# The MLP's second matrix product by two levels of seven products, with its weight operands formed during the attention

## The chip, the cores and the metric

The kernel is one program on one NeuronCore of a Trainium2 chip. The metric is the time of one execution on the device in microseconds (us). Three runs of the kernel before took 3018.52, 3020.32 and 3024.05 us; the median is 3020.32. All data are float32.

A core has a matrix engine (TensorE, PE in the profile; the loads of its stationary operand are listed as PEld), a vector engine (VectorE, DVE), a scalar engine (ScalarE, ACT), a general engine (GpSimd, POOL) and an engine that here only issues transfers (SyncE, SP). Each has its own queue and works through it in order. They meet through semaphores. SBUF is the working memory with 128 partitions, PSUM holds the results of matrix products, and DRAM holds inputs, outputs and scratch tensors.

## The reference

Two layers. The first is a graph attention over 4 x 1024 rows of 512 features with 20 key rows per batch; nothing in it is changed. The second is a transformer block on the result, conditioned by a vector per batch:

```python
mod = jax.nn.silu(c) @ W_mod + b_mod
sh_msa, sc_msa, g_msa, sh_mlp, sc_mlp, g_mlp = jnp.split(mod, 6, axis=-1)
x = x + g_msa * _attention(_modulate(_layernorm(x), sh_msa, sc_msa), W_qkv, W_out, b_out)
x = x + g_mlp * _ff(_modulate(_layernorm(x), sh_mlp, sc_mlp), W1, b1, W2, b2)
# _ff: gelu(x @ W1 + b1) @ W2 + b2, W1 512 x 2048, W2 2048 x 512
# _modulate: x * (1 + scale) + shift; 16 heads of 64; 4 batches of 1024 rows
```

The change is about `@ W2`, a product of 4096 x 2048 by 2048 x 512.

## The kernel before

**Stages.** The graph attention takes the first part, layer 1's attention the middle (about 471 to 2236 us of the profiled execution), the MLP the rest. The attention is a loop over `NS` = 256 steps. Beside each step's score and value products a planner places other work: `add(lo, hi, units, place, f, ...)` appends a task with the steps between which it is due, its share of a step and a rank in it. `emit` takes the tasks out at their steps and so fixes each engine's order. With every step POOL scales the softmax weights (L1219), DVE transposes them (L1228), SP writes them to DRAM (`wd`) and loads them back as `wT` for the value product (L1101).

**Products with seven parts.** Where a product has a 2 x 2 block form, `seven` and `with_four` (L558 to L610) form it from seven products of sums of blocks instead of eight of blocks (Strassen's method in Winograd's arrangement). Four PSUM banks `ma`, `mb`, `mc`, `md` take the seven in the order a, c, b, a2, b2, d, b3. Between them ACT copies `ma` into `mb` and `mc` into SBUF, and DVE forms `md` from `mb` and that copy (`start_d`, L585) and the last result from the same (`last`, L589); `done` takes each finished quarter. A product that reads a bank which another engine writes waits for it; `start_d` must be over before b2, `last` before b3.

**The MLP.** The rows are taken in `NB2` = 8 blocks k of 512 rows (`VB` = 4 tiles of 128). A block has two stages. In the up stage four units p, one level of seven each, form gelu(x @ W1 + b1) into `hs[p]`. A product is four matmuls of 128x256, and in this trace each float32 matmul appears as two records. ACT applies gelu from PSUM (L699), and `up_sums(p)` forms on DVE the sums of blocks of `hs` that the next stage needs (four operations of 128x512 into `hx[p]` and in place, L542 to L545). The down stage forms the block's `@ W2` by one level of seven: 16 matmuls of 128x256 a product, left operand from `hs` or `hx`, right operand a block of `w2s` (W2 in SBUF, four loads of 1 MB, L1601) or a sum of blocks `w2x` (formed once on DVE, eight operations of 128x1024, L550, in block 0). `dn_done` (L1687 to L1698) multiplies a quarter by the gate (L1690) and adds it to the rows (L1695); finished rows go out by SP.

Beside that, for the next block: `norm_load` fetches its rows (tile `xl`, queue SP) ahead of the up stage. `norm_rows` normalizes them on DVE behind unit 2 (L425). `between`, behind the first down product, transposes them in blocks of 32 on DVE (`norm_turn`, L465), and 16 transfers of 64 KB each place them in `hT`. In `between` the block's own rows are loaded too, and POOL adds the bias to them (L1680). `modulated`, behind the fourth product, applies scale and shift on ACT (`norm_mod`, L479), and POOL forms the sums of blocks of `hT` (`mlp_rows`, L550). Block 0 differs: its first two units run in the last steps of the attention, and the loads of `w2s` stand in SP's queue ahead of the rows of block 1.

Of the kernel before, what the change touches and what calls it, by code (L numbers as in the profile page):

```python
# [12 lines left out]
F32 = mybir.dt.float32  # L13
# [6 lines left out]
P = 128  # L20
# [21 lines left out]
def cond_block_kernel(  # L42
# [86 lines left out]
    x2d = [tc.dram_tile([P, F], F32, name=f"x2d{i}") for i in range(NTA)]  # L129


    with ExitStack() as gctx:
# [279 lines left out]
        def norm_load(st, k):  # L412
            for i in range(k * VB, (k + 1) * VB):
                t = rp.tile([P, F], F32, name="xl", tag="xl", bufs=VB)
                nc.sync.dma_start(t, NORM[st][0][i])
                xl[st, i] = t
# [44 lines left out]
        def norm_turn(st, k, n, home):  # L461

            hT[st, k] = hT[st, 0]
            t = home(n)
            nc.vector.transpose(  # L465
                t.rearrange("p (m k) -> p m k", k=RB),
                xl.pop((st, k * VB + n)).rearrange("p (m k) -> p m k", k=RB),
            )
            for u in range(P // RB):
                at = n * P + u * RB  # L470
                nc.sync.dma_start(hT[st, k][:, :, at : at + RB], t[RB * u : RB * (u + 1), :])

        def norm_mod(st, k, c):

            sh, sc = NORM[st][4:]
            b = k * VB // NT
            o = hT[st, k][:, c, :]
            scale, shift = modT[:, sc + c, b : b + 1], modT[:, sh + c, b : b + 1]
            nc.scalar.activation(o, o, AF.Identity, scale=scale, bias=shift)  # L479
# [74 lines left out]
        def sums_b(*args):  # L554
            for f in steps_b(*args):
                f()
# [111 lines left out]
        def mlp_rows():  # L668

            h = hT[1, 0]  # L670
            if "mlp" not in tx:
                tx["mlp"] = xp.tile([P, 6, F], F32, name="tx", tag="tx")
            o = [tx["mlp"][:, k, :].rearrange("p (c r) -> p c r", c=2) for k in range(3)]
            sums_b(nc.gpsimd, o, h[:, :2, :HB], h[:, :2, HB:], h[:, 2:, :HB], h[:, 2:, HB:])
# [26 lines left out]
        def up_sums(p):  # L701
            h = [hs[p][:, 2 * k : 2 * k + 2, :] for k in range(4)]
            sums_a(nc.vector, [hx[p][:, k] for k in range(3)], *h)


# [273 lines left out]
    with ExitStack() as actx:  # L979
# [273 lines left out]

        fill = []
# [5 lines left out]
        def add(lo, hi, units, place, f, *args):  # L1260
            fill.append((lo, hi, units, place, lambda: f(*args)))
# [96 lines left out]
        add(3, 3, 0, 4, rstd, rs1, mv1, nm1, NT, NTA)  # L1358

# [22 lines left out]
        add(NS - 8, NS - 8, 0, 4, mlp_rows)  # L1382
# [203 lines left out]
    with ExitStack() as mctx:  # L1586
# [12 lines left out]
        w2s = [mp2.tile([P, 4, F], F32, name=f"w2_{k}") for k in range(4)]  # L1599
        for k in (0, 2, 1, 3):  # L1600
            nc.sync.dma_start(w2s[k], w2[k * F : (k + 1) * F, :].rearrange("(c p) f -> p c f", p=P))  # L1601
        w2x = [mp2.tile([P, 3, 4, HB], F32, name=f"w2x{k}") for k in range(2)]
        for p in range(4):
            hx[p] = mp2.tile([P, 3, 2, HB], F32, name=f"hx{p}")
# [6 lines left out]
        gate2, bias2 = (tx["mlp"][:, k, :] for k in (3, 4))  # L1611

        def dn_lhs(which, t, c):
            p, q = divmod(c, 2)
            rows = slice(t * P, (t + 1) * P)
            at = {4: 0, 5: 1, 2: 2}.get(which)
            if at is not None:
                return hx[p][:, at, q, rows]
            return hs[p][:, 2 * {0: 0, 1: 1, 6: 2, 3: 3}[which] + q, rows]

        def dn_rhs(which, t, c):
            k, r = divmod(c, 4)
            at = {4: 0, 5: 1, 3: 2}.get(which)
            if at is not None:
                return w2x[k][:, at, r, :]
            h, f = {0: (0, 0), 1: (1, 0), 2: (1, 1), 6: (0, 1)}[which]
            return w2s[2 * h + k][:, r, f * HB : (f + 1) * HB]
# [4 lines left out]
        rows2 = {}  # L1632
        NB2 = NTA // VB
        for k in range(NB2):
# [4 lines left out]
            for p in range(2 if k == 0 else 0, 4):  # L1639
# [10 lines left out]
                if k > 0:  # L1650
                    up_sums(p)
                elif p == 3:
                    sums = []
                    for j in range(2):
                        o = [w2x[j][:, n] for n in range(3)]
                        q, r = w2s[j], w2s[2 + j]
                        sums.append(steps_b(nc.vector, o, q[:, :, :HB], q[:, :, HB:], r[:, :, :HB], r[:, :, HB:]))
                    for n, two in enumerate(zip(*sums)):
                        for f in two:
                            f()  # L1660
                        if n == 0:
                            up_sums(p)
                if p == 1 and k == 1:
                    rstd(rs2, mv2, nm2, 3 * NT, NTA)
                if p == 2 and nxt < NB2:
                    norm_rows(1, nxt)

            def between():
                if nxt < NB2:
                    for n in range(VB):  # L1670
                        norm_turn(1, nxt, n, lambda n: short() if n % 2 else tx["mlp"][:, 5, :])
                if k * VB % NT == 0:
                    spread(2, b, gate2)
                    spread(3, b, bias2)
                for n in range(VB):
                    i = k * VB + n
                    rows2[n] = rp.tile([P, F], F32, name="x2", tag="xl", bufs=VB)
                    nc.sync.dma_start(rows2[n], x2d[i])
                for n in range(VB):
                    nc.gpsimd.tensor_tensor(rows2[n], rows2[n], bias2, ALU.add)  # L1680

            def modulated():
                for c in range(FC):
                    norm_mod(1, nxt, c)
                mlp_rows()

            def dn_done(i, j, t):  # L1687
                y = t if (i, j) == (1, 1) else short()
                g = gate2[:, j * HB : (j + 1) * HB].unsqueeze(1).to_broadcast([P, 2, HB])
                nc.vector.tensor_tensor(  # L1690
                    y.rearrange("p (t f) -> p t f", t=2), t.rearrange("p (t f) -> p t f", t=2), g, ALU.mult
                )
                for n in range(2):
                    o = rows2[2 * i + n][:, j * HB : (j + 1) * HB]
                    nc.vector.tensor_tensor(o, o, y[:, n * HB : (n + 1) * HB], ALU.add)  # L1695
                    if (i, j) in ((0, 1), (1, 0)):
                        at = k * VB + 2 * i + n
                        nc.sync.dma_start(out[at * P : (at + 1) * P, :], rows2[2 * i + n])  # L1698

            steps = with_four(  # L1700
                get=dn_banks.get, short=short, lhs=dn_lhs, rhs=dn_rhs, nk=MC // 2, room=None, done=dn_done
            )
            for n, f in enumerate(steps):
                f()
                if n == 0:
                    between()
                if n == 3 and nxt < NB2:
                    modulated()
# [60 lines left out]
```

## Time and profile before

| | |
|---|---|
| median of three runs | 3020.32 us |
| profiled execution: its time, its span | 3032.2 us, 3030.2 us |
| granted TensorE clock, mean | 0.997 |
| PE busy | 2995.2 us, 99% |
| DVE, ACT, POOL busy | 67%, 48%, 44% |
| DMA: moved, mean rate | 425.25 MB, 140 GB/s |
| one MLP block, from one first down product to the next | 96.7 us |
| of it the seven down products | 7 x 6.91 us |

The page of a profile names groups of instructions by line, engine, operation, tiles and shape; each has its busy time, the mean of one in ns, and the idle time before it with what ended it. The chain of waits is followed back from the last instruction: start, length, engine, tile and line of each step. A timeline lists instructions in order with start and length (x n for a run of equal ones). A table of windows gives each engine's busy time in stretches of time. In the transfer view, digits are the busy tenths of the DMA engines in equal slices, with the GB/s moved under them.

### The profile page before, as it was taken

Reading aid. Unit: us, or ns where it says so; the run is one execution under the profiler, and the core shown is the slowest. Engines: PE = TensorE matmul, PEld = TensorE weight load, DVE = VectorE, ACT = ScalarE, POOL = GpSimd, SP = SyncE. Lnnn points to the kernel's source line nnn. Section 1 sums busy time; section 2 is a strip of 40 time slices with the busy share of each in tenths; the row PEclk is TensorE's granted clock in tenths of the full one; section 3 lists DMA queues with packets and bytes.
Section 4 is the critical chain, followed back from the end, with each engine's and each line's share of the span. In section 5 each row is a group of like instructions: output and inputs, shape, how many; then the busy total and the mean of one; then the engine's idle time right before and its main releaser. Section 6 shows DMA issues by size and latency. Waiting matters only on the chain.

```text
span 3030.2 us, 41832 instructions
## 1 busy us (share of the span) xinstructions
PE 2995.2 (99%) x15205; PEld 1969.9 (65%) x15205; DVE 2018.4 (67%) x2852; ACT 1441.5 (48%) x2380; POOL 1339.4 (44%) x922
## 2 busy tenths in 40 slices
PE   9999999999999999999999999999999999999999
PEld 6666665565555555555565555555568888888888
DVE  3788867787878877878887878887865332233222
ACT  2344456555755555755555755556641322222211
POOL 1444456555665655665665575664641101110110
PEclk8999999999999999999999999999999999999999
DMA  6343437776877776867776877876764212212020
GB/s 193 118 131 117 136 99 188 167 173 157 204 169 191 191 175 151 209 167 194 190 173 151 206 168 184 198 175 153 190 177 127 49 32 60 56 35 56 29 63 14
DMA packets 341833, 425.25 MB, mean 140 GB/s; under 512 B 88105, under 2 KB 160229, under 8 KB 341629
## 3 DMA queue, kind: packets, MB, share of 16 engines
q1 hardware_dynamic: 341392, 422.37, 55.2%
q8 instruction: 122, 2.00, 0.3%
q14 instruction: 83, 0.67, 0.1%
q10 hardware_dynamic: 236, 0.20, 0.0%
HBM read 120.93 MB, written 25.76 MB: 48 GB/s over the span
## 4 chain that ended last, share of the span: by engine, by line
PE 81%; DVE 7%; POOL 3%; issue 3%; DMA 3%; ACT 2%; SPq 2%; POOLq 0%; DVEq 0%; ACTq 0%
PE q L571 18%; PE psc L1193 14%; PE pav L1101 13%; PE pu L1176 6%; PE mbd L571 5%; PE mbu L571 5%; PE mad L571 4%; PE mau L571 3%; PE mdd L571 2%; PE mcd L571 2%; PE mdu L571 2%; PE mcu L571 2%; DVE mx L1204 1%; DMA wT<-wd 1%; POOL t L780 1%
## 5 line engine op out<-in xcount | busy, mean ns | idle before, releaser
L1219 POOL TENSOR_SCALAR w<-w,sm 128x1024 f32<-128x1024 f32 x256 | 727.8, 2843 | 705.7 <-DVE sm L1215 692.8
L1210 ACT ACTIVATE w<-psc,mx 128x1024 f32<-128x1024 f32 x512 | 570.2, 1114 | 642.8 <-DVE mx L1204 641.6
L1228 DVE STREAM_TRANSPOSE wd<-w 128x1024 f32<-128x1024 f32 x512 | 632.2, 1235 | 110.4 <-ACT w L1217 99.2
L1204 DVE TENSOR_REDUCE mx<-psc 128x1 f32<-128x1024 f32 x512 | 599.3, 1210 | 80.6 <-PE psc L1193 77.4
L1193 PE MATMUL psc<-kT,qT 64*128 64x512 f32 x2048 | 528.0, 615 | 3.6 <-ACT kT L1061 1.4
L1101 PE MATMUL pav<-wT,v 128*64 128x256 f32 x4096 | 482.3, 383 | 2.3 <-DMA wT<-wd 2.0
L1101 PEld LDWEIGHTS pav<-wT,v 128*64 128x64 f32 x4096 | 292.7, 137 | 228.3 <-issue 87.2
L1193 PEld LDWEIGHTS psc<-kT,qT 64*128 64x128 f32 x2048 | 200.2, 186 | 224.0 <-issue 151.4
L1680 POOL TENSOR_TENSOR x<-x,tx 128x512 f32<-128x512 f32 x32 | 39.9, 1279 | 616.9 <-DMA x<-x2d 616.9
L1217 ACT ACTIVATE w<-w,sm 128x1024 f32<-128x1024 f32 x256 | 291.0, 1137 | 0.0
L1185 DVE TENSOR_TENSOR xr<-pu,xr 128x512 f32<-128x512 f32 x210 | 143.6, 684 | 79.7 <-PE pu L1176 79.5
L571 PE MATMUL q<-hT,wqk 128*128 128x512 f32 (+1 forms) x396 | 181.2, 581 | 1.0 <-DVE q L585 1.0
L757 PE MATMUL pa<-kp,sfT 128*128 128x320 f32 x512 | 143.5, 433 | 1.4 <-ACT sfT L732 1.4
L593 ACT COPY mbu<-mau 128x512 f32<-128x512 f32 x30 | 17.1, 570 | 238.9 <-PE mau L571 238.9
L571 PEld LDWEIGHTS q<-hT,wqk 128*128 128x128 f32 x396 | 74.7, 190 | 80.9 <-issue 78.3
L571 PE MATMUL q<-tx,ex 128*128 128x512 f32 (+1 forms) x264 | 123.5, 591 | 1.6 <-POOL tx L656 1.6
L757 PEld LDWEIGHTS pa<-kp,sfT 128*128 128x128 f32 x512 | 94.8, 190 | 38.2 <-ACT sfT L732 1.9
L717 PE MATMUL pf<-wx,xT 128*128 128x512 f32 x256 | 116.0, 597 | 0.0
L571 PE MATMUL mad<-w,hs 128*128 128x256 f32 x512 | 113.1, 379 | 0.0
L571 PEld LDWEIGHTS mad<-w,hs 128*128 128x128 f32 x512 | 97.3, 190 | 13.2
L1176 PE MATMUL pu<-wout,oT 128*128 128x256 f32 x360 | 98.4, 396 | 4.6 <-DVE xr L1185 3.9
L1176 PEld LDWEIGHTS pu<-wout,oT 128*128 128x128 f32 x360 | 62.5, 189 | 59.1 <-issue 31.2
(308 smaller groups left out, 4576.5 us busy)
## 6 DMA issues: line engine op xcount, KB each, us to landing
wT<-wd SPq DMA_DIRECT2D x1024, 256.0 KB
wqk<-in_w_qkv SPq DMA_DIRECT2D x64, 256.0 KB
xT<-in_xt SPq DMA_DIRECT2D x32, 256.0 KB
xs<-in_x SPq DMA_DIRECT2D x32, 256.0 KB
x1d<-xs SPq DMA_DIRECT2D x32, 256.0 KB
xl<-x1d SPq DMA_DIRECT2D x32, 256.0 KB
wv<-in_w_qkv SPq DMA_DIRECT2D x32, 256.0 KB
xr<-x1d SPq DMA_DIRECT2D x32, 256.0 KB
```

The lines of the kernel that those rows point to most:

```text
L571: nc.tensor.matmul(t[:, q * width : (q + 1) * width], lhsT=lhs(which, q, k), rhs=rhs(which, q, k), start=(fresh and q == 0 and k == 0), st ...
L717: nc.tensor.matmul(pfs[i], lhsT=xT[i][:, c, :], rhs=wx[:, c, :], start=False, stop=(c == FC - 1), skip_group_check=True,)
L757: nc.tensor.matmul(pas[i][:, n, :HF], lhsT=sfT2[i][:, c, :], rhs=kp[:, b, c, n * HF : (n + 1) * HF], start=False, stop=(c == FC - 1), skip ...
L1101: nc.tensor.matmul(po[j * D : (j + 1) * D, :], lhsT=vt[b, g][:, m, p * P + j * D : p * P + (j + 1) * D], rhs=w[:, j, :, m, :], start=(m == 0),
L1176: nc.tensor.matmul(pu[0][:, q * HB : (q + 1) * HB], lhsT=a[:, q * P : (q + 1) * P], rhs=r, start=(bool(fresh) and q == 0), stop=True, skip ...
L1185: nc.vector.tensor_tensor(o, pu[0].rearrange("p (r f) -> p r f", r=2), o, ALU.add)
L1193: nc.tensor.matmul(sc[j][:, n * F : (n + 1) * F], lhsT=qT[b, gp][q, t * P : (t + 1) * P], rhs=kT[b, gp][q, n * F : (n + 1) * F], start=Tru ...
L1204: nc.vector.tensor_reduce(mx, sc, axis=AX.X, op=ALU.max, negate=True)
L1210: nc.scalar.activation(w, sc, AF.Exp, bias=mx, accum_out=sm)
L1217: nc.scalar.mul(w, w, sm)
L1219: nc.gpsimd.tensor_scalar(w, w, sm, None, ALU.mult)
L1228: nc.vector.transpose(wd[j][:, :, at, :], wn.pop((b, gp, t, j)).rearrange("p (m k) -> p m k", k=U))
```

## The change

Each of the seven products of the down stage (a group, loop variable n, in the order ORD) is itself formed by seven products, so that a block has 49 products of four matmuls 128x128. The right operands of all 49, products of sums on both levels, are formed once and kept in DRAM (`w2d`, 7 groups of 1.835 MB; `WC` = 32 columns, `WN` = 4 strips). In the attention 16 pieces of W2 are loaded (262 KB), widened to 49 strips of 32 columns by eight subtractions each on POOL (`w2_sum`), and stored (803 KB); the pieces use the memory of `xl`, which becomes one tile of four rows' size. In the MLP each of the seven groups of a block loads its operand into one of three buffers `w2r` (`load_w2`, on SP, two groups ahead). The left operands of the inner level (`inner_sums`, four operations of 128x256 for each half) are formed a group ahead, one half on DVE between the products, the other on POOL. Groups take the two sets of banks in turn. `sink` gathers the 49 results in `du`, `d5`, `dv` and `d3`; `scale` applies the gate, `to_rows` adds to the rows, partly on POOL. The fourth operation of `up_sums` becomes `up_sums4` and moves into the down stage (two on POOL, two on DVE). The transposes of the next block's rows move from the down stage to the up stage, behind unit 2; their transfers to `hT` (`norm_place`) start the down stage. `mlp_rows` is done in two halves in groups 5 and 6. The sums `w2x` and the resident `w2s` are gone. The host lays W2 out for the pieces.

```diff
+    w2d = tc.dram_tile([7, P, 4 * WN * 7 * WC], F32, name="w2d")
         def norm_load(st, k):
-            for i in range(k * VB, (k + 1) * VB):
-                t = rp.tile([P, F], F32, name="xl", tag="xl", bufs=VB)
-                nc.sync.dma_start(t, NORM[st][0][i])
+            t = rp.tile([P, VB, F], F32, name="xl", tag="xl", bufs=1)
+            for n in range(VB):
+                nc.sync.dma_start(t[:, n, :], NORM[st][0][k * VB + n])
...
-        def norm_turn(st, k, n, home):
+        def norm_turn(st, i, spare):
+            t = spare if i % VB == 0 else xl[st, i - 1]
             nc.vector.transpose(
...
+        def norm_place(st, i):
+            t = turned.pop(i)
             for u in range(P // RB):
+                at = i % VB * P + u * RB
+                nc.sync.dma_start(hT[st, 0][:, :, at : at + RB], t[RB * u : RB * (u + 1), :])
...
         def up_sums(p):
-            sums_a(nc.vector, [hx[p][:, k] for k in range(3)], *h)
+            nc.vector.tensor_tensor(o1, a21, a22, ALU.add)
+            nc.vector.tensor_tensor(o2, o1, a11, ALU.subtract)
+            nc.vector.tensor_tensor(a21, a11, a21, ALU.subtract)
+        def up_sums4(e, p):
+            e.tensor_tensor(hx[0][:, p], hs[p][:, 2:4, :], hx[1][:, p], ALU.subtract)
...
+        def w2_load(n):
+            t = rp.tile([P, VB * F], F32, name="w2g", tag="xl", bufs=1)
+            w2g[n] = t[:, : 49 * WC].rearrange("p (j i f) -> p j i f", j=7, i=7)
+            nc.sync.dma_start(w2g[n][:, :4, :4, :], w2[n])
+        def w2_sum(n, k):
+            def at(m):
+                return w2g[n][:, m, :4, :] if k < 4 else w2g[n][:, :, m, :]
+            o, i, j = ((4, 1, 0), (5, 3, 4), (1, 3, 1), (6, 2, 5))[k % 4]
+            nc.gpsimd.tensor_tensor(at(o), at(i), at(j), ALU.subtract)
...
+        for n in range(4 * WN):
+            at = (n // 6 * 64) + 4 + n % 6 * 7
+            add(at, at, 0, 0, w2_load, n)
+            for k in range(8):
+                add(at + 1 + k // 2, at + 1 + k // 2, 0, 4, w2_sum, n, k)
+            add(at + 6, at + 6, 0, 0, w2_store, n)
...
-        w2s = [mp2.tile([P, 4, F], F32, name=f"w2_{k}") for k in range(4)]
+        w2r = [mp2.tile([P, 4, WN, 7, WC], F32, name=f"w2r{k}") for k in range(3)]
+        ORD = (0, 4, 1, 5, 6, 2, 3)
+        def load_w2(g):
+            if g < 7 * NB2:
+                at = PLACE[ORD[g % 7]]
+                nc.sync.dma_start(w2r[g % 3].rearrange("p r n i f -> p (r n i f)"), w2d[at])
+        for g in range(3):
+            load_w2(g)
...
+            def product(t, which, fresh=False):
+                for k in range(4):
+                    nc.tensor.matmul(
+                        t.rearrange("p (n f) -> p n f", n=WN),
+                        lhsT=lhs(which, *divmod(k, 2)),
+                        rhs=w2r[g % 3][:, k, :, PLACE[which], :],
...
+            return (
+                (lambda: product(a, 0, True), lambda: nc.scalar.copy(b, a)),
+                (lambda: product(c, 4, True), lambda: nc.scalar.copy(s5, c)),
+                (lambda: product(b, 5), lambda: nc.vector.tensor_tensor(d, b, s5, ALU.add)),
+                (lambda: product(a, 1), lambda: done(0, 0, a)),
+                (lambda: product(b, 6), last),
+                (lambda: product(d, 2), lambda: done(0, 1, d)),
+                (lambda: product(b, 3), lambda: done(1, 0, b)),
+            )
...
                 for n, f in enumerate(steps):
                     f()
+                    if p == 3 and n in (2, 4):
+                        for f in inner_sums(nc.vector, 7 * k, n // 2 - 1):
+                            f()
+                    if p == 3 and n == 2:
+                        for f in inner_sums(nc.gpsimd, 7 * k + 1, 0):
+                            f()
...
                 if p == 2 and nxt < NB2:
                     norm_rows(1, nxt)
                     for n in range(VB):
+                        norm_turn(1, nxt * VB + n, spare)
+                if p == 0 and k > 0:
+                    load_w2(7 * k + 2)
...
+            for n, which in enumerate(ORD):
+                g = 7 * k + n
+                if n > 0 and g + 2 < 7 * nxt + 2:
+                    load_w2(g + 2)
+                after_v, after_a = [], []
+                if n == 0 and nxt < NB2:
+                    for i in range(VB):
+                        norm_place(1, nxt * VB + i)
+                if n == 2:
+                    rows2 = rp.tile([P, VB, F], F32, name="x2", tag="xl", bufs=1)
+                    for i in range(VB):
+                        nc.sync.dma_start(rows2[:, i, :], x2d[k * VB + i])
+                if 0 < n < 6:
+                    after_v += inner_sums(nc.vector, g + 1, 0)
+                    for f in inner_sums(nc.gpsimd, g + 1, 1):
+                        f()
+                if n == 2:
+                    for p in range(2):
+                        up_sums4(nc.gpsimd, p)
+                if n == 3:
+                    after_v += [lambda p=p: up_sums4(nc.vector, p) for p in range(2, 4)]
+                    with_bias(0)
+                    if nxt < NB2:
+                        after_a = [lambda c=c: norm_mod(1, nxt, c) for c in range(FC)]
+                if n == 4:
+                    nc.vector.tensor_tensor(d3, du, d5, ALU.add)
+                    after_v.append(lambda: scale(0, dv))
+                    with_bias(1)
+                if n == 5:
+                    after_v.append(lambda: nc.vector.tensor_tensor(d5, du, d5, ALU.add))
+                    if nxt < NB2:
+                        mlp_rows(0)
+                if n == 6:
+                    scale(1, d3)
+                    scale(1, d5)
+                    to_rows(nc.gpsimd, 0, 1, d3)
+                    to_rows(nc.gpsimd, 1, 1, d5)
+                    if nxt < NB2:
+                        mlp_rows(1)
+                    after_v.append(lambda: to_rows(nc.vector, 0, 0, dv))
+                    after_v.append(lambda: rows_out2(0))
+                steps = inner(g, (dn_banks, up_banks)[n % 2], done, room)
+                for m, (f, after) in enumerate(steps):
+                    f()
+                    after()
+                    for _ in range(-(-len(after_v) // (7 - m))):
+                        after_v.pop(0)()
+                    if m > 1 and after_a:
+                        after_a.pop(0)()
+            scale(0, du)
+            to_rows(nc.vector, 1, 0, du)
+            rows_out2(1)
```

## The prediction

> **What bounds the kernel now.** First the page, for the span and for the share of each engine:
>
> ```profile
> span 3030.2 us, 41832 instructions
> PE 2995.2 (99%) x15205; PEld 1969.9 (65%) x15205; DVE 2018.4 (67%) x2852; ACT 1441.5 (48%) x2380; POOL 1339.4 (44%) x922
> ...
> L1219 POOL TENSOR_SCALAR w<-w,sm 128x1024 f32<-128x1024 f32 x256 | 727.8, 2843 | 705.7 <-DVE sm L1215 692.8
> ```
>
> TensorE is the bound, and POOL waits 2.7 us (692.8 / 256) for its softmax factor in each attention step. Then the chain of waits and the stretches of one MLP block, k=1, at the start of its down stage:
>
> ```profile
> 2396.75 6.91 PE mad L571 x32
> 2403.66 6.91 PE mcd L571 x32
> ...
> 2438.19 6.91 PE mbd L571 x32
> 2493.45 6.91 PE mad L571 x32
> ```
>
> ```profile
> 2300.00:2349.00 49.00, 49.00 (x229) 43.14 (x228) 22.92 (x26) 4.92 (x8) 10.88 (x8) 1.00 0.30 65
> 2397.00:2445.00 48.00, 48.00 (x224) 42.24 (x223) 9.82 (x18) 4.71 (x8) 9.88 (x8) 1.00 0.26 55
> ```
>
> (The columns behind the length: busy PE, PEld, DVE, ACT, POOL, granted clock, DMA share, GB/s.) Seven down products of 6.91 us follow one another, 48.35 us of a period of 96.70, PE has no gap, DVE and POOL are busy about 10 of 48 us each and the DMA moves 55 GB/s. So a shorter down stage is worth all it saves, as long as the other engines keep up. Next, the timelines: what a narrow product takes, and how DVE and POOL get on.
>
> ```profile
> 2011.84 1.95 PE L571 MATMUL q<-wv,hT 128*128 128x128 f32 x16
> 2013.62 1.03 PE L1176 MATMUL pu<-wout,osum 128*128 128x256 f32 x4
> ```
>
> ```profile
> 2335.36 1.46 DVE L1690 TENSOR_TENSOR s<-s,tx 128x512 f32<-128x512 f32 x1
> 2336.92 2.71 DVE L1695 TENSOR_TENSOR x<-x,s 128x256 f32<-128x256 f32 x2
> 2341.54 0.69 DVE L1690 TENSOR_TENSOR s<-mdd,tx 128x512 f32<-128x512 f32 x1 [1.90 <-PE mdd L571]
> ```
>
> ```profile
> 2335.00 1.27 POOL L550 TENSOR_TENSOR tx<-hT,tx 128x512 f32<-128x512 f32 x1
> 2336.23 1.71 POOL L550 TENSOR_TENSOR hT<-hT 128x512 f32<-128x512 f32 x1
> 2337.90 1.45 POOL L550 TENSOR_TENSOR tx<-hT,tx 128x512 f32<-128x512 f32 x1
> ```
>
> Sixteen 128x128 records start within 1.78 us, 0.111 each. And beside POOL, L1690 with two operands in SBUF takes 1.46 us, while with one in PSUM it takes 0.69; L1695 takes 2.71 for two, while 54 of its 64 take 0.42 each, away from POOL. A VectorE operation with two SBUF operands is held until the running POOL operation ends. This reading decides the forecast.
>
> **The change, part by part.** The sum is made against the profiled execution, 3032.2 us, which is 11.9 above the median of the runs, 3020.3; that is taken off at the end. About 0.2%, 6 us, is what a measurement tells from no change.
>
> *Products.* Down has 49 products of 4 matmuls, 196 of 128x128, two records each: 392 x 0.112 = 43.9 us (0.001 kept for joins) in place of 48.35, so -4.45 per block, -35.6 for eight. Upper end: the chain gives some 16-matmul products of this shape 3.77 us for 32 records, 0.118 each, so 46.2 and -2.15. That the right operand is now read in four strips of 32 no row shows; it is within these ends. A narrower product is suspect by a rule of the Trainium skill ("TensorE: Matmul & The Clock Gate", Back-to-back issue gap): in a stream with weight loads it gives 81 ns a matmul at 128 columns and 131 at 512, 2.5 times as much per column; with that ratio the narrow form would lose. The rows here decide otherwise: 0.111 at 128 against 0.216 at 256 (6.91 / 32).
>
> *Joins.* A product lasts 0.89 us instead of 6.91. `start_d` reads the third product and must end before the fifth; it has the fourth as cover. From the rows: PE's end to DVE's start 0.20, the operation about 0.29 (0.69 for 512 and 0.42 for 256 continued to 128), DVE's end to PE with its weight load 0.155: 0.65 of 0.89, so 0.25 to spare. The same holds for `last` ahead of the seventh product: 14 such places a block. ACT's copy ahead of the third product (about 0.25, from 570 for 512 and 359 for 256) has the same cover and 0.3 to spare; the four L479 of 0.80 us in group 3 stand between such copies. I cost ACT at nothing; uncovered they would be 0.5 each.
>
> *DVE and POOL in the down stage.* POOL now gets, per block, 20 inner sums of 0.73 (rows L542 to L545, 128x256) and twelve operations of 1.27 (two fourth sums, four biases, two row sums, four for the rows): 29.8 of 43.9 us, where it had 10. DVE gets about 25, of which 30 operations have two SBUF operands and stand in one queue with `start_d` and `last`. I placed both queues in time by hand, with the durations above and the hold. Group 4, from its first product: the sums left over from group 3 end at 0.9; the add into d3 meets a POOL inner sum and ends at 2.1, not 1.6; two inner sums alternate with POOL's and end at 3.0 and 3.8; `start_d` runs 3.8 to 4.1 instead of 2.9 to 3.2; the fifth product, due at 3.58, starts at 4.28: 0.7 lost. Its `last` loses another 0.4 behind the same pairs. Group 6: two scales end at 2.2; POOL's row sum has started, so DVE's row sum ends near 3.9 and `start_d` at 4.2: 0.8 lost. Groups 0, 3 and 5 lose about 0.15 to 0.2 each. Together 2.4 a block, 19.2 in all. Lower end 0 (the operations happen to interleave); upper end all 14 places late by one held operation, 1.0 less 0.25: 10.5 a block. I take the walk.
>
> *Rows turned beside the first matrix.* Before, at block 1:
>
> ```profile
> 2386.39 1.91 DVE L425 TENSOR_SCALAR xl<-xl,mv,rs 128x512 f32<-128x512 f32 x4
> 2389.95 0.70 DVE L585 TENSOR_TENSOR mdu<-mbu,s 128x512 f32<-128x512 f32 x1 [1.66 <-PE mbu L571]
> ```
>
> DVE has 1.66 us left ahead of unit 3's L585. Four transposes (708 and 670 ns alternately, 0.63 apart) add 2.55; one of four sums, 0.61, leaves: L585 is 0.28 late, and an up product of 1.73 us covers 0.68. POOL's four inner sums (2.9 us) start just there. If they hold the sum ahead of L425 alone, 0.4 us of PE is lost; if they hold L425 too, 2.0. No row shows L425 beside POOL. It runs 512 elements at 0.46 apart, faster than the two-operand form (0.61), so I lean to the upper end: 1.5 in six blocks, 9. The Trainium skill ("SBUF — State Buffer", Who interferes with whom) says that tensor_scalar in a two-port mode contends with GpSimd; by it 12 would stand here.
>
> *Start of the MLP.* SP issues three loads of 1.835 MB instead of four of 1.05 ahead of the next rows' loads: 1.31 MB more.
>
> ```profile
> DMA  0007167998989998999999999999721000000000
> GB/s 0 0 0 289 38 200 232 330 318 245 271 261 384 379 325 223 376 364 397 392 399 405 399 399 376 392 382 394 269 82 38 3 0 0 0 0 0 0 20 0
> ```
>
> (Slices of 0.8 us from 2268.) The DMA is full there, near 392 GB/s: 3.3 us later. L425 ran 2291.43 to 2293.95 and held L585 until then; now it ends near 2297.3, the transposes add 2.55, and PE, which lost 0.3 there, loses 6 more; POOL's hold adds 0.5. I take 6.5, ends 3 (the loads share the queue better) and 9 (two more joins late). The eight w2x sums of 1.22 us go, beside PE: nothing.
>
> *W2's stream.* Six loads fall in one down stage: 11.0 MB, with rows 1.05, output 1.05 and hT 1.05. At 392 GB/s and 157 for hT's 128-byte runs (an estimate from the packets of the trace) that is 28 + 5.4 + 6.7 = 40 of 43.9 us: covered, barely. SP issues the 16 hT loads (0.67 us each, 10.7) ahead of group 1's load, which has 8 us left of its 12.5 and needs 4.7 and its latency. From then on 8.4 MB are due within 27 us, so 310 GB/s is the least. Cost 0; without that rate see the rivals. hT lands before the ACT operations of group 3; the rows' POOL operations end beside the first up products.
>
> *Pieces in the attention.* POOL: 64 operations of 128 and 64 of 224 elements, about 0.46 and 0.66 (from 0.73 and 1.27 for 256 and 512): 72 us, 1.1 in each of 64 steps, against 2.7 idle. Uncovered, 72. The DMA is 74% busy at 179 GB/s in 471 to 2236; 17 MB more go in. SP can be held by a piece's load until the store before it has landed, with the wT loads behind it; PE lost only 2.0 us to wT in all. Ends 0 and 48 (16 holds of 3 us); I take 3, nearer to the row of PE's waits.
>
> Sum: -35.6 + 19.2 + 9 + 6.5 + 3 = +2.1; 3032.2 + 2.1 - 11.9 = **3022**.
>
> **The rivals.**
> - *POOL does not get in the way* (joins met, up 0.4, start 3, attention 0): -35.6 + 2.4 + 3 = -30, so 2990. For it: the tasks alternate between product steps. Against it: 30 operations in a queue with 0.25 to spare.
> - *The hold is deeper*: half of the upper end, 5.2 a block, +22: 3045; all of it, 3087. It decides against the change from 2.7 a block on.
> - *W2's stream is too slow*: one mechanism on the other side. At 262 GB/s (2270 to 2280, mixed with stores) 8.4 MB take 32 us instead of 27: 5.3 a block, 42 in all, so 3065. From 310 GB/s down it costs. Against it: 376 in 2280 to 2290.
> - *The pieces delay the attention*: SP's holds reach wT, or POOL's sums the chain w, transpose, wT: half of 48, 3045.
> - *The products don't get shorter as said*: 0.118 a record: +18, so 3041.
>
> **How the numbers follow.** The likeliest case, hold as walked, 0.42, has its own range 3008 to 3036 (down 1.2 to 3.6 a block, up 0.4 to 2.0); of it a fifth lies under 3014, 0.45 within 6 us, the rest above. No hold 0.20; deeper hold 0.12; stream 0.14; attention 0.07; narrow products 0.05. Faster: 0.20 + 0.09; same 0.20; slower the rest, 0.51. The range 2988 to 3070 leaves out the lower part of the second case and the upper ends of stream and hold, 0.18.
>
> **What would show it.** Right: down products of about 0.9 us, 45 to 47 us from a block's first to its last; PE idle ahead of the fifth product of groups 4 and 6, released by DVE; inner sums on DVE with a mean well above 0.42; at the start, PE idle about 6 us behind L425's and the transposes' lines. Wrong: PE's waits on a w2r load (stream), or on wT in the attention (pieces); L425's mean at 0.54 beside POOL with no gap at unit 3; a down stage near 44 us.

## The result and the profile after

The changed kernel takes 3041.74 us (median of 6 runs, 3037.79 to 3044.75) beside 3020.45 us of the kernel before (6 runs): a ratio of 1.007, with a 95% interval of 1.0057 to 1.0083. It is 21.3 us slower. Its profiled execution has a span of 3040.4 us, near its median.

The page of the profile after:

```profile
span 3040.4 us, 45804 instructions
PE 2971.8 (98%) x16549; PEld 1979.5 (65%) x16549; DVE 2239.5 (74%) x3308; ACT 1475.5 (49%) x2524; POOL 1622.0 (53%) x1274
...
L1234 POOL TENSOR_SCALAR w<-w,sm 128x1024 f32<-128x1024 f32 x256 | 728.2, 2845 | 648.9 <-DVE sm L1230 630.4
...
L1116 PE MATMUL pav<-wT,v 128*64 128x256 f32 x4096 | 493.2, 386 | 15.1 <-DMA wT<-wd 13.7
```

PE is busy 23 us less than before (13 less than in a second profile of the kernel before) and is yet done later: it now stands idle. The last line gives a first reason. PE's wait for `wT` in the attention was 2.0 us in all and is 13.7 now. (Line numbers are those of each profile's own kernel: L571, L585, L589 and L425 of the kernel before are L579, L593, L597 and L428 in the changed one, and some experiments move the later ones by one.)

To see where the time lies, I cut each profile's span into three stretches by PE's timeline, from the first score product to the last, from there to the first down product, and from there to the end. The kernel before was profiled a second time for this.

| profile | first to last score product | to the first down product | to the end |
|---|---|---|---|
| before | 1818.5 | 62.6 | 730.3 |
| before, second profile | 1815.3 | 63.0 | 730.3 |
| after | 1838.0 | 69.7 | 723.9 |

The attention takes 19.5 us more than in the first profile (22.7 more than in the second), the start of the MLP 7.1 more, and the rest of the MLP, which was to gain, 6.4 less. The sum, 20, is the 21.3 of the runs within their scatter. (The first score product comes at 418.8 us in the first profile of before, so the attention begins earlier than the 471 given above. What comes ahead of it took 10 us longer in that profile; the last section has it.)

In the MLP PE's waits and a whole block stand so, in the table of waits from 2412 us on and in the table of windows:

```profile
PE mbu L579 <- DVE mdu L593: 6.9, 5, 1.4
PE mbd L1704 <- DVE mdd L1721: 5.8, 13, 0.6
PE mbd L1704 <- DVE s L1715: 1.5, 7, 0.2
```

```profile
2412.70:2509.00 96.30, 93.78 (x618) 86.79 (x617) 57.73 (x104) 26.59 (x65) 36.90 (x36) 1.00 0.55 184
```

(us in all, times, longest; the columns of the table of windows are those named in the prediction.) Every wait of PE is for DVE: for L593, the `start_d` of an up unit, and for the two operations at the joins of the inner products, `start_d` (L1721) and `last` (L1715). A steady block takes 96.15 us from one first down product to the next, 96.70 before. No wait for a `w2r` load appears, and the DMA moves 184 GB/s at a share of 0.55.

The place of the largest gap in a down stage, group 6 of block 1, in the timelines of DVE, POOL and PE:

```profile
2454.87 1.76 DVE L1792 TENSOR_TENSOR x<-x,dv 128x512 f32<-128x512 f32 x1
2456.55 0.28 DVE L1721 TENSOR_TENSOR mdd<-mbd,s 128x128 f32<-128x128 f32 x1
```

```profile
2454.43 1.65 POOL L1792 TENSOR_TENSOR x<-x,tx 128x512 f32<-128x512 f32 x1 [1.95 <-DVE tx L1788]
2456.03 1.72 POOL L1792 TENSOR_TENSOR x<-x,d 128x512 f32<-128x512 f32 x1
```

```profile
2455.28 1.06 PE L1704 MATMUL mad<-w2r,hs 128*128 128x128 f32 x8
2456.89 1.16 PE L1704 MATMUL mbd<-w2r,hy 128*128 128x128 f32 x8 [0.56 <-DVE mdd L1721]
```

DVE's row sum, two operands in SBUF, takes 1.76 us instead of the 0.69 of its kind, because POOL's row sum started 0.4 us before it. `start_d` stands behind it and takes its 0.28, and PE's fifth product, which would follow the fourth after 0.89, starts after 1.61.

And unit 3's gap, block 1:

```profile
2401.59 3.13 DVE L428 TENSOR_SCALAR xl<-xl,mv,rs 128x512 f32<-128x512 f32 x4
2404.65 0.70 DVE L469 STREAM_TRANSPOSE tx<-xl 128x512 f32<-128x512 f32 x1
2405.38 2.21 DVE L469 STREAM_TRANSPOSE xl<-xl 128x512 f32<-128x512 f32 x3
2407.51 0.67 DVE L593 TENSOR_TENSOR mdu<-mbu,s 128x512 f32<-128x512 f32 x1
```

```profile
2399.96 2.30 POOL L1682 TENSOR_TENSOR hy<-hx 128x256 f32<-128x256 f32 x2 [35.87 <-PE mbu L579]
2402.21 0.90 POOL L1682 TENSOR_TENSOR hy<-hy,hx 128x256 f32<-128x256 f32 x1
2403.20 0.79 POOL L1682 TENSOR_TENSOR hy<-hx,hy 128x256 f32<-128x256 f32 x1
```

The four L428 took 1.91 us together before and take 3.13 beside POOL's inner sums.

### The profile page after: what moved, and what is told of

Its sections match the earlier page's. It is cut to its first block, busy times and chain, and to the rows that moved or that the text cites. A ratio compares the mean times of both kernels' runs of the same rounds, so it can differ in the third digit from the quotient of the medians.

```text
span 3040.4 us, 45804 instructions
## 1 busy us (share of the span) xinstructions
PE 2971.8 (98%) x16549; PEld 1979.5 (65%) x16549; DVE 2239.5 (74%) x3308; ACT 1475.5 (49%) x2524; POOL 1622.0 (53%) x1274
## 4 chain that ended last, share of the span: by engine, by line
PE 69%; DVE 14%; DMA 4%; ACT 4%; SPq 4%; issue 3%; POOL 3%; DVEq 0%; POOLq 0%; ACTq 0%
PE q L579 17%; PE psc L1208 13%; PE pav L1116 12%; PE pu L1191 5%; PE mbu L579 4%; SPq L1247 3%; PE mau L579 2%; DMA wT<-wd 2%; PE mbd L1704 2%; DVE hy L1682 2%; DVE mx L1219 2%; ACT w L1225 2%; PE mdu L579 2%; PE mcu L579 1%; POOL t L795 1%
## 5 line engine op out<-in xcount | busy, mean ns | idle before, releaser
L1116 PE MATMUL pav<-wT,v 128*64 128x256 f32 x4096 | 493.2, 386 | 15.1 <-DMA wT<-wd 13.7
L1682 POOL TENSOR_TENSOR hy<-hx 128x256 f32<-128x256 f32 x48 | 44.8, 947 | 349.4 <-PE mbu L579 251.0
L579 PE MATMUL q<-hT,wqk 128*128 128x512 f32 (+1 forms) x396 | 181.2, 581 | 1.0 <-DVE q L593 1.0
L579 PEld LDWEIGHTS q<-hT,wqk 128*128 128x128 f32 x396 | 74.7, 190 | 80.9 <-issue 78.2
L579 PE MATMUL q<-tx,ex 128*128 128x512 f32 (+1 forms) x264 | 123.5, 591 | 1.7 <-POOL tx L664 1.2
L814 POOL TENSOR_TENSOR wts<-t,sm 128x640 f32<-128x640 f32 x32 | 40.7, 1271 | 124.0 <-DVE sm L812 116.2
L1225 ACT ACTIVATION_READ_ACCUMULATOR w<-psc,mx 128x1 f32 x512 | 98.7, 193 | 0.0
L579 PE MATMUL q<-wv,hT 128*128 128x128 f32 x768 | 94.4, 276 | 0.9 <-DVE q L593 0.9
```

Of the source, the lines that this page charges most:

```text
L579: nc.tensor.matmul(t[:, q * width : (q + 1) * width], lhsT=lhs(which, q, k), rhs=rhs(which, q, k), start=(fresh and q == 0 and k == 0), st ...
L1116: nc.tensor.matmul(po[j * D : (j + 1) * D, :], lhsT=vt[b, g][:, m, p * P + j * D : p * P + (j + 1) * D], rhs=w[:, j, :, m, :], start=(m == 0),
L1225: nc.scalar.activation(w, sc, AF.Exp, bias=mx, accum_out=sm)
```

## The experiments

**Where the attention loses.** Compared step by step (from one score product's first record to the next step's), the two profiles differ by more than 2 us in three of 256 steps only: step 28 of batches 0, 1 and 2, by 6.9, 5.4 and 4.7 us. Batch 3, which has no pieces, loses nothing. In each of batches 0 to 2 a piece is loaded at step 25. SP's timeline and waits of the kernel after, and PE's timeline, for batch 0:

```profile
588.37 1.26 SPq L1286 DMA_DIRECT2D w2d<-w2g  x1
595.43 0.58 SPq L1274 DMA_DIRECT2D w2g<-in_w  x1
596.11 4.15 SPq L1247 DMA_DIRECT2D wT<-wd  x4
```

```profile
SPq L1274 <- DMA w2d<-w2g: 39.9, 8, 6.1
```

```profile
604.74 0.65 PE L1116 MATMUL pav<-wT,v 128*64 128x256 f32 x2
609.00 6.27 PE L1116 MATMUL pav<-wT,v 128*64 128x256 f32 x30 [3.62 <-DMA wT<-wd]
615.20 1.98 PE L579 MATMUL q<-tx,wqk 128*128 128x512 f32 x4
```

SP issues the store of the old piece, then stands 5.7 us at the new piece's load until that store has landed, since both use one tile; the `wT` loads are behind it. PE waits 3.62 us for one of them. Then its value product takes 6.27 us instead of 3.6, and that is the granted clock, as the table of windows shows for these steps:

```profile
605.00:609.00 4.00, 0.38 (x3) 0.03 (x1) 4.00 (x6) 0.00 (x0) 3.35 (x2) 0.81 0.60 144
609.00:615.30 6.30, 6.30 (x31) 3.90 (x31) 3.99 (x6) 3.43 (x5) 6.22 (x8) 0.58 0.85 175
```

The same product in the experiment without POOL's work (below), after a wait as long but with the clock at 1.00 in the windows from 613.6 to 624 us, takes its old length:

```profile
617.36 3.64 PE L1116 MATMUL pav<-wT,v 128*64 128x256 f32 x30 [3.73 <-DMA wT<-wd]
```

In batches 1 and 2 the waits are 3.19 and 2.41 us, and the products take 5.25 and 5.33 at a clock of 0.69. So of the 19.5 us, 11.7 are longer waits for `wT`, and about 6 are these three products at the lower clock; 2 lie elsewhere. Two runs test the hold against the bytes and POOL's work, and against a cause outside the pieces.

*Pieces ten steps apart:*

```diff
-            at = (n // 6 * 64) + 4 + n % 6 * 7
+            at = (n // 4 * 64) + 4 + n % 4 * 10
```

> The changed kernel with four pieces of W2 in each batch of 64 attention steps, ten steps apart, in place of six, seven apart. The same loads, sums and stores, so the same bytes and the same work on POOL; only the next piece's load now stands four steps, not one, behind the store before it. Theory A (SP waits in order for the store to land, with the wT loads behind it): no long step at step 28 of a batch, the attention from the first to the last score product falls from 1738 us to about 1721 (it was 1718 before the change), and the time from 3041.7 to about 3025. Rival B (the bytes, or POOL's sums, delay the wT chain): the attention stays at 1735 to 1738 and the time at 3038 to 3042.

(The lengths of the attention in this text are each 100 us too low by a slip in a subtraction; read 1838, 1821 and 1818, and 1835 to 1838 for the rival. Their differences stand.) Measured: 3024.09 us, ratio 1.0005 (0.9996 to 1.0014) to the kernel before. The attention takes 1817.7 us, and step 28 has its old length. SP's wait for the store is gone from the table of waits, and PE's for `wT` is 2.1. Theory A holds. The same bytes and the same sums cost nothing that shows once the load does not stand behind a store in flight. The granted clock is 1.00 throughout this attention. (The run moves the stores too; that the loss hangs on the hold and not on where a store's bytes fall is read from the chain of waits of the kernel after, which runs from the store through SP's held load and the `wT` loads to the late value product.)

*The kernel before, with the pieces formed and not used:*

```diff
+        for n in range(4 * WN):
+            at = (n // 6 * 64) + 4 + n % 6 * 7
+            add(at, at, 0, 0, w2_load, n)
+            for k in range(8):
+                add(at + 1 + k // 2, at + 1 + k // 2, 0, 4, w2_sum, n, k)
+            add(at + 6, at + 6, 0, 0, w2_store, n)
```

> The kernel before with the pieces of W2 loaded, summed and stored in the attention at the changed kernel's steps, and never used; its MLP is the old one. It does one part of the change alone. Theory A: all that the pieces cost lies in the attention and is there without the new MLP: about 19.5 us more than the kernel before, 3040. Rival: the attention's loss comes with the changed memory layout or the planner's new order and not with the pieces: under 5 us more.

Measured: 3041.16 us, ratio 1.0058 (1.0042 to 1.0075); attention 1838.1, the rest 62.9 and 730.3 as before. SP waits 39.7 us in 8 holds for the stores, and PE 14.3 for `wT`. So this part alone costs what the whole change costs, and the new MLP together with its start comes out even. (The three tasks are those of the changed kernel. The kernel also takes over the one tile for `xl`; that the layout is not the cause is shown by the run before, which has it too.)

**The start of the MLP.** *The rows of block 1 ahead of the second and third operand load:*

```diff
-        for g in range(3):
-            load_w2(g)
+        load_w2(0)
...
             if nxt < NB2:
                 norm_load(1, nxt)
+            if k == 0:
+                load_w2(1)
+                load_w2(2)
```

> The changed kernel with the rows of block 1 loaded ahead of the second and third load of W2's operands, not behind them. Theory: the rows land about 9 us earlier, DVE's normalizing and transposes are over before the fourth product of unit 3 ends, PE does not stand idle there (4.3 us now), so the granted clock, 0.53 in the 5.5 us after that idle time, stays at 1.00; together 6 to 9 us less, 3033 to 3036. Rival 1: the clock falls there anyway, then 4 to 5 us less. Rival 2: the second and third load now come too late for groups 1 and 2, PE waits on w2r, and nothing is gained: 3040 to 3044.

Measured: 3034.30 us, ratio 1.0038 (1.0023 to 1.0053), 7.4 less than the changed kernel. The number is the theory's, but the profile is nearer to rival 1: from the last score product to the first down product 65.7 us instead of 69.7, so 4.0 of the gain is here, 1.6 in the rest of the MLP and 2.5 in the attention, where nothing was changed and profiles of kernels with pieces seven steps apart scatter from 1832.6 to 1842.3. The fifth product no longer waits, but the last one of the unit does, as PE's timeline shows, and the clock falls all the same:

```profile
2302.93 1.89 PE L579 MATMUL mdu<-hT,ex 128*128 128x256 f32 x8
2307.02 3.38 PE L579 MATMUL mbu<-tx,w 128*128 128x256 f32 x8 [2.20 <-DVE hs L597]
```

```profile
2302.00:2307.00 5.00, 2.82 (x14) 2.13 (x12) 4.97 (x8) 0.24 (x2) 3.54 (x4) 1.00 0.61 85
2307.00:2310.40 3.40, 3.38 (x9) 2.73 (x10) 3.10 (x7) 1.63 (x4) 0.00 (x0) 0.57 0.57 78
```

In the first of these two windows POOL is busy 3.54 of 5 us with its inner sums, and DVE 4.97: L597 is late in DVE's queue there. No wait on `w2r` took its place, so rival 2 falls.

**POOL beside DVE.** *POOL's work in the MLP left out from block 1 on:*

```diff
-                    for f in inner_sums(nc.gpsimd, g + 1, 1):
+                    for f in inner_sums(nc.gpsimd, g + 1, 1) if k == 0 else ():
                         f()
...
-                    to_rows(nc.gpsimd, 0, 1, d3)
-                    to_rows(nc.gpsimd, 1, 1, d5)
+                    if k == 0:
+                        to_rows(nc.gpsimd, 0, 1, d3)
+                        to_rows(nc.gpsimd, 1, 1, d5)
```

(and the fourth sums, the bias, the rows' sums and group 1's inner sums on POOL in the same way)

> The changed kernel without POOL's work in the MLP from block 1 on (half of the inner sums, two fourth sums, the bias, two row sums, the sums of the rows), so the output is not the reference's; DVE's, ACT's and PE's instructions are all kept. Theory (DVE's operations with two operands in SBUF are held by POOL's): L1682 on DVE falls to about 0.42 us, PE's gaps ahead of the fifth and seventh products and in unit 3 go, a block from 96.1 to about 92.3 us; seven down stages at 2.2 and six up stages at 1.65 make 25 us less, 3016. Rival (DVE's queue is too full by itself for joins of 0.89 us): the gaps stay, and the time is within 5 us of 3041.7.

Measured: 3017.13 us, ratio 0.9985 (0.9975 to 0.9995). From block 1 on, PE has no wait at all in the trace; a block takes 92.1 us, and the MLP from the first down product on 698.0 instead of 723.9. Two groups of DVE in the kernel after, from 2316 us on, and the same two in this one:

```profile
L1682 DVE TENSOR_TENSOR hy<-hx 128x256 f32<-128x256 f32 x48 | 34.1, 750 | 0.0
...
L428 DVE TENSOR_SCALAR xl<-xl,mv,rs 128x512 f32<-128x512 f32 x24 | 18.8, 842 | 0.0
```

```profile
L1682 DVE TENSOR_TENSOR hy<-hx 128x256 f32<-128x256 f32 x48 | 20.1, 460 | 0.0
...
L428 DVE TENSOR_SCALAR xl<-xl,mv,rs 128x512 f32<-128x512 f32 x24 | 11.5, 542 | 0.0
```

DVE has the same instructions in both and keeps up when POOL is silent. So its queue is not too full by itself; from block 1 on the hold is the whole loss. (The profiled execution is the slowest of this kernel's runs; it has the same slow first stage as the first profile of the kernel before.)

*DVE's side work behind the joins,* all of POOL's work kept:

```diff
-                    for _ in range(-(-len(after_v) // (7 - m))):
+                    for _ in range(min(len(after_v), {2: 1, 4: 3, 5: 9}.get(m, 0))):
                         after_v.pop(0)()
...
-                    scale(1, d3)
-                    scale(1, d5)
-                    to_rows(nc.gpsimd, 0, 1, d3)
-                    to_rows(nc.gpsimd, 1, 1, d5)
-                    if nxt < NB2:
-                        mlp_rows(1)
+                    def gate_rows2(i, y):
+                        scale(1, y)
+                        to_rows(nc.gpsimd, i, 1, y)
+                    after_v.append(lambda: gate_rows2(0, d3))
+                    after_v.append(lambda: gate_rows2(1, d5))
+                    after_v.append(lambda: scale(0, dv))
```

(`scale(0, dv)` leaves group 4 for group 6, and `mlp_rows(1)` follows the groups.)

> The changed kernel with DVE's side work in the down stage put behind the two operations that PE waits for: of each group's inner sums and other tasks one behind start_d, three behind last, the rest behind the sixth product, none ahead of start_d; in group 6 the scales and row sums likewise, POOL's part of the row sums behind its scale, and the last half of the rows' sums on POOL behind the groups. Same work on every engine. Theory (what costs is only a held operation that stands in DVE's queue ahead of start_d or last): a down stage from 46.1 to about 44.3 us, 1.8 a block, 15 us in all, 3026 to 3028; unit 3's loss of 1.65 stays. Rival (DVE has no time left beside POOL, so the loss only moves): PE waits for an inner sum or for a later join instead, within 5 us of 3041.7.

Measured: 3031.48 us, ratio 1.0031 (1.0018 to 1.0043), 10.3 less. The steady block goes to 94.2 us, 1.95 less, as expected. From the first down product to the end it is 712.2 us, 11.7 less instead of 15: the last two down stages go only from 45.9 to 44.9, and what follows the last product grows from 5.6 to 7.5, since the gate and the row sums of the last block now stand behind it. Its PE waits from 2420 us on:

```profile
PE mbu L579 <- DVE mdu L593: 6.9, 5, 1.4
PE mbu L1704 <- ACT s L1720: 0.7, 2, 0.4
PE mbd L1704 <- DVE mdd L1721: 0.7, 2, 0.4
PE mbu L1704 <- DVE hy L1682: 0.5, 3, 0.2
```

The waits at the joins fall from 7.8 us (5.8, 1.5 and 0.5, with L1715 of both banks) to 0.7. What comes next are an inner sum on DVE and ACT's copy into `s5` (L1720), at 0.4 us at most. In the steady blocks the loss has not moved elsewhere.

*The halves of group 1's inner sums exchanged,* so that POOL rests while DVE normalizes:

```diff
-                    if p == 3 and n == 2:
-                        for f in inner_sums(nc.gpsimd, 7 * k + 1, 0):
+                    if p == 3 and n == 5:
+                        for f in inner_sums(nc.vector, 7 * k + 1, 0):
                             f()
...
-                    for f in inner_sums(nc.vector, 7 * k + 1, 1):
+                    for f in inner_sums(nc.gpsimd, 7 * k + 1, 1):
                         f()
```

> The changed kernel with the halves of group 1's inner sums exchanged: DVE forms the half that is ready early, behind the sixth product of unit 3, and POOL the other at the start of the down stage, so that POOL rests while DVE normalizes and transposes the next rows. Theory (POOL's four inner sums hold L428 and the sum ahead of it): L428 falls from 0.78 to about 0.46 apart, unit 3 starts its fifth product on time in six blocks, 1.65 each, 10 us less, 3031 to 3033. Rival (the four transposes alone make unit 3 late): the gap stays at over 1 us, and the time within 4 us of 3041.7.

Measured: 3036.50 us, ratio 1.0045 (1.0027 to 1.0063), 5.2 less, with runs from 3027.41 to 3039.12. That misses the expected 10. In the trace the mechanism is as expected: L428 is back at 1.91 us for four, PE's wait for L593 is gone in all steady blocks, though the four transposes stay, and from the first down product to the end it is 713.3 us, 10.6 less. The runs scatter by 12 us, and their mean granted clock goes with it: 0.998 in the fastest, 0.996 to 0.997 in the others. The profiled one is the fastest, with an attention of 1832.6 us, while the profiled one of the experiment before took 3035.45 with 1842.3. So the single gains of a few us, taken from medians of kernels with pieces seven steps apart, are uncertain by some us; the lengths in the traces are the better measure of each.

**All four edits together.**

> The four edits together: pieces spaced ten steps, rows of block 1 first, DVE's side work behind the joins, group 1's halves exchanged. If the four losses are separate places on PE's path, their gains add: 17.6 (spacing) and 7.4 (rows first), as measured, 15 (joins) and 10 (halves) as expected, 50 of 3041.7: 2990 to 2994, 1% less than the kernel before. If they cover for one another, 3000 to 3010.

Measured: 2995.28 us, ratio 0.9914 to the kernel before, 0.9899 to 0.9929: 25 us faster than before and 46 faster than the change as it was made. It is 1 us above the expected band. The four single gains as measured add to 40.6, a little less than together, so the losses don't cover for one another. The three stretches are 1819.4, 62.2 and 701.7 us. The attention and the rest of the MLP are separate places: the last stretch gains 22.2, where the joins and the halves alone gave 11.7 and 10.6. At the start of the MLP two edits help one another: rows first alone gave 4.0 and the exchanged halves 0.2, together they give 7.5, PE has no wait for L593 or L597 there any more, and the clock stays at 1.00. A steady block in the table of windows, and PE's longest kinds of wait in the whole MLP:

```profile
2476.20:2568.80 92.60, 92.46 (x619) 86.51 (x619) 55.95 (x105) 26.54 (x65) 36.46 (x36) 1.00 0.55 185
```

```profile
PE mbu L1703 <- ACT s L1719: 1.5, 4, 0.4
PE mbu L1664 <- DVE xr L1146: 0.9, 1, 0.9
PE mbd L1703 <- DVE mdd L1720: 0.7, 1, 0.7
```

**The kernel before, once more.**

> The kernel before, profiled once more. Its first profile reached the first score product of the attention at 419 us from the span's start, the changed kernel's at 409, with the same work up to there. If that is a scatter of the first stage and not of the kernel, this profile reaches it near 409, with a span near 3020; if it belongs to the kernel before, near 419 again.

Measured: one run of 3019.46, with a span of 3017.5; the first score product comes at 408.8 us. The 10 us were a scatter of the first stage, not the kernel's.

The attention's length sorts all profiles: 1838.0, 1838.1, 1835.5, 1842.3, 1832.6 and 1836.8 with pieces seven steps apart (after and five experiments), 1818.5, 1815.3, 1817.7 and 1819.4 without them or with ten. In the first six the traces have PE at half clock for 13.7, 6.8, 10.2, 17.1, 3.4 and 6.8 us of the attention, in the other four not at all; the shortest and the longest of the six are those with the least and the most of it, so a good part of their scatter is the clock.

## Why the prediction was right, and where it was not

The range (2988 to 3070) and the likelier sign, slower, held. The forecast of 3022 was 20 us short, and the likeliest case's own range, 3008 to 3036, was missed by 6. The term that was mis-sized is *pieces in the attention*: 3 taken, 19.5 measured. That the sign came out is in part luck: the likeliest case stood at +2.1, about the same time, and it was a case with a chance of 0.07 that made the change slower. The three terms of the steady MLP (products, joins, rows turned) were right as a sum, -7.4 predicted and -6.4 measured.

- **Products.** Predicted 0.112 us a record, 43.9 a down stage. Where nothing waits, products follow at 0.893 for 8 records, 0.112 each, and without POOL a down stage takes 43.8 us up to the next up product. Right; the four strips of 32 cost nothing that shows.
- **Joins.** The walk put 0.7 us at group 4's fifth product, 0.4 at its seventh, 0.8 at the fifth of group 6. The gaps, with the 0.10 by which the next product is longer, are 0.62, 0.48 and 0.82. A steady down stage takes 46.15 us, so 2.25 above the 43.9 predicted and 2.4 above the 43.8 without POOL, where 2.4 were taken. (That the hold decides against the change from 2.7 a block on does not follow from the prediction's own terms: by them it is even at 2.1 and 6 us slower at 2.9. Nothing else rests on it.) That the hold and not DVE's load is the cause is shown by the run without POOL.
- **Rows turned beside the first matrix.** 1.5 taken between 0.4 and 2.0; measured 1.65 in each of six blocks. The open question was whether L428 is held by POOL; it is, 0.78 apart instead of 0.46. So the rule of the Trainium skill ("SBUF — State Buffer", Who interferes with whom) that tensor_scalar can contend with GpSimd agrees with this trace. The 2.0 that was worked out for it was a little high, since POOL's sums do not cover all four. The transposes alone cost nothing, as worked out.
- **Start.** 6.5 taken, 7.1 measured, but not by the steps named. The rows waited for the DMA as said, but less: L428 starts 11.0 later than before, behind an attention that ended 9.6 later, so 1.4 and not 3.3. With the transposes behind it L593 is 4.3 later, and PE waits 4.3 us, not 6. The rest is the clock, at about half after that wait, which was not in the sum: the size came out right by luck, with a part that was too large and one that was missing.
- **W2's stream.** Costed at 0 and measured at 0: no wait for `w2r` in any profile's table of waits.
- **Pieces.** The mechanism was written down, SP held by a piece's load until the store has landed, with the `wT` loads behind it, and with its price: 16 holds of 3 us at most, half of it as a rival with 3045 and a chance of 0.07. I took 3 by the row of PE's waits for `wT`, 2.0 us in all. That row tells that `wT` came in time before; it does not tell by how much. The holds were 8, of 5 us on average and up to 6.1, and the three at the loads of step 25 cost 4.7 to 6.9 each at step 28. About 6 of the 19.5 us are the lower clock behind these three waits, a price that the prediction did not have at all. The row to look at was SP's own timeline: at which steps its `wT` loads stand, and which piece's load falls ahead of them.
- **The sum.** With the measured term in place of mine the forecast would be about 3039, 3 short of the measured time.

The other rivals: no hold (2990) is what the kernel without POOL's work shows in the MLP, and the changed kernel does not. A deeper hold, the slow stream and the slower products did not come about.

## What to carry to other kernels

When work is moved into a stretch where the queue that issues transfers is on the way of something urgent, place its waiting instructions by that queue's timeline: a load that reuses a buffer whose store is in flight stops everything behind it, and here the same bytes cost nothing that shows ten steps apart. Price a wait of the matrix engine at more than its length: behind waits of 2.2 to 4.3 us the clock often fell, for 1.6 to 3 us more each. When a product gets shorter, count what the other engines may be late by before it waits, and put operations that can be held (two SBUF operands, or tensor_scalar, beside a busy POOL) behind the operation that the product waits for, never ahead; moving tasks in this way was worth 10 us, without any work taken away. Four small losses can hide a gain that the change really has: here 25 us net, once they were found one by one.

## What the runs showed of the hardware that was not expected

The granted clock can fall after a short wait of PE. In the table of windows of the kernel after, around the wait of 4.3 us at the start of the MLP:

```profile
2304.00:2309.00 5.00, 0.73 (x3) 0.49 (x2) 4.77 (x8) 0.84 (x2) 0.00 (x0) 0.83 0.36 63
2309.00:2314.50 5.50, 5.50 (x15) 4.33 (x15) 5.43 (x9) 0.00 (x0) 3.94 (x4) 0.53 0.44 62
```

The granted clock is 0.53 for 5.5 us after the wait. Most of the next 15 matmul records start 0.43 us apart instead of 0.216, which costs about 3 us more than the wait itself. After a wait of 2.2 us (rows first) it was 0.57 for 3.4 us; after waits of 1.4 us in the steady blocks it stayed at 1.00. In between the length alone does not decide: in the attention it fell after waits of 2.41, 3.19 and 3.62 us (kernel after), and stayed at 1.00 after 3.44 (kernel before with pieces) and 3.73 (without POOL's work). The Trainium skill ("TensorE: Matmul & The Clock Gate", What's actually happening) puts the fall at an idle window of about 3.4 us. The 4.3 us agrees; the 2.2 us is shorter than that, the 3.73 without a fall is longer, and the measurement decides. What decides in between stays open here.

The stage ahead of the attention took 8 to 10 us longer in some profiles than in others of the same or of equal work there: the first score product came at 418.8 us in the first profile of the kernel before, at 416.9 in that of the kernel without POOL's work, at 408.8 in the second profile of the kernel before and at 408.9 in the changed kernel's. The granted clock makes most of it. The two profiles of the kernel before in the table of windows, first the first:

```profile
17.00:34.00 17.00, 17.00 (x68) 13.56 (x67) 1.82 (x6) 1.48 (x3) 0.00 (x0) 0.50 1.03 352
17.00:34.00 17.00, 16.80 (x104) 12.73 (x104) 5.16 (x13) 4.00 (x9) 0.00 (x0) 1.00 1.04 356
```

In the first one PE works at 0.50 for these 17 us; the same instructions are 1.75 us late at 16 us from the start, 9.9 at 38 us, and stay so. Why the clock stayed low there for 17 us is open. It means that the difference between two profiled spans (10.2 us here) can be far from that of the medians (21.3), and that stretches with equal ends should be compared instead.
